# Expert tiles of the last routing round in pairs that share their weights, and a second table pass for the rest, in a two-layer Perceiver kernel

## The chip, the cores and the metric

The kernel runs on one core of a Trainium2 chip, as one program. Five engines take part, each with its own instruction queue that is worked in order: TensorE (PE, matrix products; its weight loads are listed as PEld), VectorE (DVE), ScalarE (ACT), GpSimd (POOL) and SyncE (SP, which here only issues DMAs). PE reads its operands from the on-chip buffer SBUF and writes to PSUM; DMAs move data between HBM and SBUF. The metric is the device time of one execution in microseconds; lower is better. The kernel before took 1743.54 us, the median of three runs (1740.70 to 1745.26).

## What is computed

4096 tokens (128 batches of 32) of 256 numbers go through six residual steps: cross attention to a context of 257 rows per batch, causal self attention, a feed-forward net with ternary weights, a second cross attention with 16 heads, local attention over five neighbours, and at last a mixture of experts. The change is in the last step alone. Cut to what matters it is:

```python
logits = x_flat @ router_w.T                     # 8 experts
top_v, top_i = top_k(softmax(logits), 2)         # two experts per token
top_v = top_v / sum(top_v)
for k in range(2):
    pos = (how many tokens before this one chose the same expert as their k-th)
    keep = pos < C                               # C = int(1.25 * 4096 / 8 * 2) = 1280
    expert_in[expert, pos] = layernorm(x)[token] if keep
    h = gelu(expert_in @ w1[expert])             # 256 -> 1024
    y = h @ w2[expert]                           # 1024 -> 256
    out[token] += gate * keep * y
```

All of it is in float32; the weights of one expert are two matrices of 1 MB.

## The kernel before

**Groups and lanes.** The 4096 tokens are 32 groups of 128. `group(g)` is a generator that brings one group through the five first steps and the router. Six lanes of buffers let six groups be in flight at a time.

**The order of the work** is found when the program is built. `Order` holds a set of such generators ("threads"). Each yields what it wants next: a slot of a buffer pool (`Slots`), a delay in ns, another thread's end, or an instruction block with an engine and an estimated duration. `Order.run` takes again and again the block that could begin first by these estimates, breaks ties by rank, and writes its instructions out. So the estimates (`LAG`, the price of a change of ScalarE's function table `TABLE` and `SWITCH`, `EARLY` and `LAND` for DMAs) decide the order of instructions on every engine; at run time the engines keep that order and wait for each other by semaphores. `keep_busy` puts in a few products that nobody reads where PE would idle long.

**Routing.** After every few groups (`TOGETHER`: seven times four, then two, one and one) `route(r)` finds the two experts of each token, ranks the tokens of an expert by products with a triangular matrix (`ranks`, the tile `chosen`), and works out a place in a list for each token. POOL writes (token number, gate) with an indirect DMA into the list `slot_ids` in HBM, a scatter for each of the two choices and each group. Every 128 places of an expert's list are one expert tile. `rounds_of_tiles` says how many tiles each round may start: 1, six times 8, 4, 2 and 17, together 72, whatever the routing is; `tiles_of_round` works out on VectorE which expert and which 128 places each tile of the round has (`i_exp`, `i_row`). In the last round also tiles that are not full are taken.

**An expert tile** (`expert_tile`, lines 1371 to 1453 of the kernel before) does this:

- `both_weights` takes two buffers of 1 MB from `halves_w` and POOL gathers the expert's `w1_moe` and `w2_moe` rows into them. There are three such buffers (`w`) while groups are running; when the context buffers `kT` and `kn` are used no more, six more are made of them, nine in all.
- POOL gathers the 128 list entries (`ids`), then the 128 token rows (`xt`, from `x_rows` in HBM).
- PE transposes the rows (L1408), ACT or DVE copies them to `xTm`.
- PE computes the hidden layer in two halves, each 4 blocks x 2 products of 128 columns, each followed by a Gelu on ACT (L1430) into `hT`.
- PE multiplies back: 8 products of 256 columns into one PSUM tile; ACT or DVE scales by the gate (`y`, L1449 and L1450).
- POOL scatters `y` to `out` with an add (L1129).

`xTm` and `hT` together are one slot of `rows_mid`, of which there are two, so two tiles can be between transpose and the end of the second product. There are three `xt`, eight `ids` and two `y` buffers, and four PSUM tiles.

**Locks.** Scatters and gathers of one HBM table are kept apart in the plan by the locks `at_slots`, `at_rows` and `at_out`. `locked` and `read` take the lock, then wait `EARLY` = 2500 ns, then issue; `locked` holds it for `LAND` = 4000 ns more. These are numbers of the plan; at run time POOL waits for the earlier DMA's semaphore.

A matmul in float32 of this kernel appears as two records in the trace. Line 357 (365 after the change) is the helper `matmul`, which records all products, so the groups are told apart by their tiles: `ps<-xTm,w` (or `kT`, `kn`) is the hidden layer, `ps<-w,hT` the second product.

## Time and profile before

| | |
|---|---|
| median of three runs | 1743.54 us |
| profiled execution, its own time | 1740.96 us |
| its span in the trace | 1739.3 us |
| mean granted TensorE clock | 0.957 |
| PE, DVE, ACT, POOL busy | 1574.5, 996.4, 1005.1, 773.8 us |
| DMA, mean over the span | 193 GB/s |
| last rank matmuls of the last round begin | 1520.8 us |
| last matmul ends | 1728.0 us |

The profile is of one execution; all stretches are us from the start of its span. A line of time order has start, duration, engine, line, operation, tiles written and read, partitions by elements, the count of merged instructions, and in brackets how long the engine was idle before it and what ended that, inferred from semaphore events. Where the named engine had long been done, something else was waited for, often a DMA. PE's busy time counts a record as busy from its start to its modelled end; consecutive records overlap, so pace is read from start to start. POOL's indirect DMAs are busy for as long as POOL writes out their descriptors; the data lands later.

### The profile page before, as it was taken

The numbers are of one execution on the slowest core, as the hardware profiler recorded it, in microseconds if no ns is written. First come the engines' busy times: TensorE is split into PE (matmuls) and PEld (weight loads), VectorE is DVE, ScalarE is ACT, GpSimd is POOL, SyncE is SP. The second block draws the span as 40 slices with busy tenths as digits, with TensorE's granted clock in tenths as the row PEclk, the third lists the DMA queues.
The fourth block names the chain that finished last, engine by engine and source line by source line (L and its number), as shares of the span: only waits on it lengthen the run. The fifth ranks groups of instructions, "written<-read, shape, count | busy, mean of one in ns | idle before, by whom it ended". The sixth has DMA issues, their size and how long they took to land. (4 is left out here: it accounts for less than half of the span.)

```text
span 1739.3 us, 43252 instructions
## 1 busy us (share of the span) xinstructions
PE 1574.5 (91%) x16702; PEld 1236.5 (71%) x16702; DVE 996.4 (57%) x3554; ACT 1005.1 (58%) x2649; POOL 773.8 (44%) x1026
## 2 busy tenths in 40 slices
PE   6988888899889999999999999999998998888987
PEld 5655656566667777767676777767776787877976
DVE  4685758777876776675667655775667443320000
ACT  1466655558666776756676666767666654312221
POOL 3221223333345435455444553454444555576763
PEclk8997989899999999999999999999999899989999
DMA  8562345353366566555655756646753357688984
GB/s 303 181 232 85 107 149 184 117 189 111 110 218 202 162 218 228 190 185 179 208 184 181 261 187 203 200 152 216 244 171 129 131 183 271 195 271 279 302 290 124
DMA packets 133150, 336.39 MB, mean 193 GB/s; under 512 B 17744, under 2 KB 43344, under 8 KB 114256
## 3 DMA queue, kind: packets, MB, share of 16 engines
q0 software_dynamic: 41984, 179.40, 31.3%
q1 hardware_dynamic: 90816, 154.09, 27.0%
q8 instruction: 132, 2.16, 0.5%
q14 instruction: 74, 0.61, 0.1%
q10 hardware_dynamic: 144, 0.13, 0.0%
HBM read 309.68 MB, written 23.87 MB: 192 GB/s over the span
## 5 line engine op out<-in xcount | busy, mean ns | idle before, releaser
L520 POOL TENSOR_SCALAR rstd<-mv 128x1 f32<-128x1 f32 x192 | 47.5, 248 | 477.9 <-DVE mv L515 357.3
L965 ACT ACTIVATE probs<-sps,nm 128x256 f32<-128x256 f32 x512 | 241.3, 484 | 29.1 <-DVE nm L921 21.1
L357 PEld LDWEIGHTS ps<-xTm,w 128*128 128x128 f32 x1632 | 209.0, 195 | 30.3 <-issue 13.5
L357 PE MATMUL ps<-xTm,w 128*128 128x128 f32 x1632 | 225.8, 283 | 5.0 <-issue 2.0
L357 PE MATMUL ps<-w,hT 128*128 128x256 f32 x768 | 203.2, 389 | 2.7 <-DVE qb L1085 1.3
L1430 ACT ACTIVATE hT<-ps 128x512 f32<-128x512 f32 x144 | 85.7, 597 | 196.5 <-PE ps L357 125.6
L919 DVE TENSOR_REDUCE nm<-sps 128x2 f32<-128x512 f32 x256 | 164.0, 683 | 34.4 <-PE sps L357 28.2
L583 PE MATMUL sps<-ident,probs 128*128 128x128 f32 x1024 | 156.9, 286 | 21.0 <-ACT probs L965 15.7
L493 ACT COPY probsT<-sps 128x512 f32<-128x512 f32 x238 | 137.7, 598 | 51.8 <-PE sps L583 45.3
L357 PEld LDWEIGHTS ps<-w,hT 128*128 128x128 f32 x768 | 134.1, 191 | 33.9 <-issue 16.6
L583 PEld LDWEIGHTS sps<-ident,probs 128*128 128x128 f32 x1024 | 120.1, 146 | 47.7 <-ACT probs L965 36.1
L1129 POOL DMA_INDIRECT out<-y,ids x72 | 117.7, 1635 | 69.5 <-ACT y L1450 33.1
L1124 POOL DMA_INDIRECT w<-in_w_moe,i_exp x99 | 101.5, 1025 | 95.1 <-PE ps L357 77.1
L493 ACT COPY xnT<-ps 128x256 f32<-128x256 f32 x173 | 64.0, 376 | 113.0 <-PE ps L535 94.0
L357 PE MATMUL sps<-probsT,kn 128*32 128x64 f32 x4096 | 108.0, 227 | 11.7 <-ACT probsT L493 6.8
L521 POOL TENSOR_TENSOR rstd<-rstd,mhalf 128x1 f32<-128x1 f32 x192 | 110.7, 577 | 16.0
L965 ACT ACTIVATION_READ_ACCUMULATOR probs<-sps,nm 128x1 f32 x512 | 109.2, 213 | 0.0
L357 PEld LDWEIGHTS sps<-probsT,kn 128*32 128x32 f32 x4096 | 71.9, 111 | 49.8 <-issue 32.2
L357 PE MATMUL sps<-kT,wide 32*64 32x256 f32 x2048 | 94.6, 420 | 6.9 <-DVE aT L998 6.8
L524 DVE TENSOR_SCALAR xn<-x,mv,rstd 128x256 f32<-128x256 f32 x175 | 72.5, 416 | 36.3 <-POOL rstd L521 35.4
L535 PE MATMUL ps<-ident,xn 128*128 128x128 f32 x384 | 76.5, 286 | 14.4 <-DVE xn L524 7.8
L1124 POOL DMA_INDIRECT xt<-x_rows,ids x72 | 71.7, 996 | 36.3 <-issue 14.0
(304 smaller groups left out, 3500.5 us busy)
## 6 DMA issues: line engine op xcount, KB each, us to landing
kT<-in_ctxT SPq DMA_DIRECT2D x256, 257.0 KB
kn<-in_ctx SPq DMA_DIRECT2D x256, 256.0 KB
x<-in_x SPq DMA_DIRECT2D x32, 128.0 KB
last<-in_ctx_last SPq DMA_DIRECT2D x32, 128.0 KB
out<-x POOLq DMA_DIRECT2D x32, 128.0 KB
x_rows<-xn POOLq DMA_DIRECT2D x32, 128.0 KB
x_rows<-nothing SPq DMA_DIRECT2D x7, 512.0 KB
w<-in_w SPq DMA_DIRECT2D x2, 1024.0 KB
```

The lines of the kernel that those rows point to most:

```text
L357: nc.tensor.matmul(out, lhsT=lhsT, rhs=rhs, **how)
L493: ("ACT", 60 + 0.815 * n, lambda: nc.scalar.copy(out, in_)),
L520: nc.gpsimd.tensor_scalar(rstd, mv[:, 1:2], EPS, None, ALU.add)
L521: nc.gpsimd.tensor_tensor(rstd, rstd, mhalf, ALU.pow)
L524: yield either(326, 1250, lambda e: e.tensor_scalar(xn, xg, mv[:, 0:1], rstd, ALU.subtract, ALU.mult))
L535: nc.tensor.transpose(pt[:, c, :], x[:, c * P : (c + 1) * P], ident)
L583: nc.tensor.transpose(by_key[:, i, c, :], e[:, i * LK + c * P : i * LK + (c + 1) * P], ident)
L919: nc.vector.tensor_reduce(nm[:, :, r], sps[r].rearrange("p (j k) -> p j k", j=2), AX.X, ALU.max)
L965: lambda: nc.scalar.activation(e[:, (2 * i + j) * LK : (2 * i + j + 1) * LK], sps[r][:, j * LK : (j + 1) * LK], AF.Exp, bias=nm[:, j, r : ...
L1124: nc.gpsimd.indirect_dma_start(out=dst, out_offset=None, in_=src, in_offset=bass.IndirectOffsetOnAxis(ap=idx, axis=0))
L1129: nc.gpsimd.indirect_dma_start(out=dst, out_offset=bass.IndirectOffsetOnAxis(ap=idx, axis=0), in_=src, in_offset=None, compute_op=op)
L1430: yield act(495, lambda: nc.scalar.activation(hT[:, 4 * half : 4 * half + 4, :].rearrange("p f t -> p (f t)"), hps, AF.Gelu), "gelu")
```

## The change

The last round's 17 tiles are no longer all alike. `rounds_of_tiles` now gives for each round a list of passes of (size, count). All rounds but the last have one pass of size 1. The last has two: four units of size 2, then nine of size 1; 8 + 9 tiles as before. A unit of size 2 (a "two" here) is 256 consecutive places of one expert.

- `tiles_of_round` runs its table of tiles once per pass. For size 2 it counts whole pairs of an expert's remaining tiles (`twos`), and makes two row indices per unit. After each pass it takes what was given out off `full`. Each pass's units are started by the new `begun`, when the slot scatters are in the plan (`sent`).
- `expert_tile` becomes `expert_tiles`. Each unit gathers the weights once. Each of its one or two sets of rows has its own id gather, row gather, transpose and copy, into one `xTm` of 256 columns. The hidden layer of a two is 16 products of 256 columns, with a Gelu after each 512 columns; the second product is done for each 128 rows, 2 x 8 products of 256 columns, side by side in one PSUM tile; two `y`, two scatters.
- Buffers: `rows_mid` are two `xTm` alone, twice as wide; `hT` becomes `hidden_of`, three halves of a hidden layer, each twice as wide, and a tile takes two of them, one when each half begins. The zero tile `nothing` is now borrowed from the `y` buffers.
- The plan: `SWITCH` 1000 to 700; `EARLY` is waited before a lock is asked for, not under it; the lags between a tile's PE blocks are 0 in the last round and 300 ns in the others (300 and 400 before).

```diff
-    per, most, pairs = [], 0, 0
-    for n in together:
+
+
+
+    per, did, pairs = [], 0, 0
+    for r, n in enumerate(together):
         pairs += 2 * n * P
-        full = max(0, pairs // TS - E + 1)
-        per.append(full - most)
-        most = full
-    per[-1] += 2 * E - 1
+        full = max(0, pairs // TS - E + 1) - did
+        if r == len(together) - 1:
+            full += 2 * E - 1
+            two = max(0, (full - E) // 2)
+            per.append([(2, two), (1, full - 2 * two)])
+        else:
+            per.append([(1, full)])
+        did += sum(size * n for size, n in per[-1])
+        per[-1] = [p for p in per[-1] if p[1]]
...
-    SWITCH = 1000.0
+    SWITCH = 700.0
...
-    rows_mid = Slots(
-        [(keep.tile([P, 2, TS], F32, name=f"xTm{i}"), keep.tile([P, 8, TS], F32, name=f"hT{i}")) for i in range(2)]
-    )
+    rows_mid = Slots([keep.tile([P, 2, 2 * TS], F32, name=f"xTm{i}") for i in range(2)])
+
+    hidden_of = Slots([keep.tile([P, 4, 2 * TS], F32, name=f"hT{i}") for i in range(3)])
...
     def locked(lock, engine, ns, emit):
 
+        yield EARLY
         yield lock
-        yield EARLY
         yield [(engine, ns, emit, None, LAND)]
         order.give(lock, None)
...
-        table = order.thread(tiles_of_round(r), order.now.rank)
+        sent = Mark()
+        table = order.thread(tiles_of_round(r, sent), order.now.rank)
         for i in range(RB):
             for k in range(2):
                 yield from locked(
                     at_slots, "POOL", 1000, lambda: scatter(slot_ids, islot[:, k, i : i + 1], ids[:, k, i, :])
                 )
         yield table
-        i_row, i_exp = table.made
-        rounds_done.append(
-            [
-                order.thread(expert_tile(r, t, i_row[:, t : t + 1], i_exp[:, t : t + 1]), tile_rank(r, t))
-                for t in range(ROUNDS[r])
-            ]
-        )
+        sent.end()
...
-        yield from steps("DVE", (850, there), (1640, sums), (1000, which), (1150, first_slots), (1290, weights))
-        order.now.made = i_row, i_exp
+        yield from steps("DVE", (850, there))
+        for size, n in ROUNDS[r]:
+            te = [P, n, E]
+            past, one = (work.tile([P, NT, E], F32, name=f"t_{x}")[:, 0:n] for x in ("past", "one"))
+            row, some = (work.tile([P, NT], F32, name=f"t_{x}")[:, 0:n] for x in ("row", "some"))
+            at_i = work.tile([P, size + 1, n], I32, name=f"at_{r}_{size}")
+            i_row, i_exp = at_i[:, 0:size], at_i[:, size : size + 1]
+            over = lambda t: t.unsqueeze(1).to_broadcast(te)
+            tiles = iota_t[:, 0:n].unsqueeze(2).to_broadcast(te)
+
+            def sums():
+                units = full
+                if size == 2:
+
+                    units = twos
+                    nc.vector.tensor_scalar(twos, full, 0.5, -0.25, ALU.mult, ALU.add)
+                    nc.vector.tensor_scalar(twos, twos, MAGIC, MAGIC, ALU.add, ALU.subtract)
+                nc.vector.tensor_copy(upto, units)
...
+                    nc.vector.scalar_tensor_tensor(row, some, float(TS), row, ALU.mult, ALU.add)
+                    nc.vector.tensor_scalar(i_row[:, 1], row, iota_p, float(NOBODY), ALU.add, ALU.add)
...
+                nc.vector.tensor_tensor(took, took, twos if size == 2 else full, ALU.min)
+                nc.vector.scalar_tensor_tensor(done, took, float(size), done, ALU.mult, ALU.add)
+                nc.vector.scalar_tensor_tensor(full, took, -float(size), full, ALU.mult, ALU.add)
+
+            yield from steps(
+                "DVE", (1640 + 150 * (size - 1), sums), (1000, which), (1150 + 150 * (size - 1), first_slots), (1360, weights)
+            )
+            order.thread(begun(r, t, size, n, i_row, i_exp, sent), order.now.rank)
+            t += size * n
+
+    def begun(r, t, size, n, i_row, i_exp, sent):
+        yield sent
+        for i in range(n):
+            order.thread(
+                expert_tiles(r, t + size * i, [i_row[:, k, i : i + 1] for k in range(size)], i_exp[:, 0, i : i + 1]),
+                tile_rank(r, t + size * i),
+            )
...
     def read(lock, dst, src, idx):
+        yield EARLY
         yield lock
-        yield EARLY
         yield [("POOL", 1000, lambda: gather(dst, src, idx), None, 0.0)]
         order.give(lock, None)
         yield LAND
...
+        N = len(i_rows)
+        between = 0.0 if r == len(ROUNDS) - 1 else 300.0
+        mid, ids = [], []
+
+        def rows_of(i):
+            mine = yield ids_of
+            yield from read(at_slots, mine, slot_ids, i_rows[i])
+            xt = yield rows_in
+            yield from read(at_rows, xt, x_rows, mine[:, 0:1])
+            ids[i] = mine
+            if i == 0:
+                mid.append((yield rows_mid))
+                known.end()
+            else:
+                yield known
+            xT = mid[0]
+            ps = yield ps_g
+            pt = ps[:, 0:D].rearrange("p (c t) -> p c t", c=2)
+
+            def turn():
+                for c in range(2):
+                    nc.tensor.transpose(pt[:, c, :], xt[:, c * P : (c + 1) * P], ident)
+
+            yield pe(221, turn)
+            order.give(rows_in, xt)
+            yield copy(xT[:, :, i * TS : (i + 1) * TS], pt, D)
+            order.give(ps_g, ps)
+
+        read_by, known = [], Mark()
+        for i in range(N):
+            ids.append(None)
+            read_by.append(order.thread(rows_of(i), order.now.rank))
+        for x in read_by:
+            yield x
+        xT = mid[0]
         yield loaded
         yield landed[0]
         wk = w1[0].rearrange("p (kc f) -> p kc f", kc=2)
+        M = N * TS
+        each = 512 // M
+        hT = []
         for half in range(2):
-            hps = yield ps_g
-            for f in range(0, 4, 2):
-                def hidden():
-                    for i in range(2):
-                        n = f + i
-                        products(
-                            hps[:, n * TS : (n + 1) * TS],
-                            [(wk[:, kc, (4 * half + n) * P : (4 * half + n + 1) * P], xT[:, kc, :]) for kc in range(2)],
-                        )
-
-                yield pe(888, hidden)
-            yield act(495, lambda: nc.scalar.activation(hT[:, 4 * half : 4 * half + 4, :].rearrange("p f t -> p (f t)"), hps, AF.Gelu), "gelu")
-            order.give(ps_g, hps)
+            hT.append((yield hidden_of))
+            for b in range(0, 4, each):
+                hps = yield ps_g
+                for f in range(0, each, 3 - N):
+
+                    def hidden():
+                        for n in range(f, f + 3 - N):
+                            at = (4 * half + b + n) * P
+                            products(
+                                hps[:, n * M : (n + 1) * M], [(wk[:, kc, at : at + P], xT[:, kc, 0:M]) for kc in range(2)]
+                            )
+
+                    yield [("PE", 757 if N == 2 else 888, hidden, None, 300.0 if f + 3 - N == each else between)]
+                out_h = hT[half][:, b : b + each, 0:M]
+                in_h = hps.rearrange("p (f t) -> p f t", f=each)
+                yield act(495, lambda: nc.scalar.activation(out_h, in_h, AF.Gelu), "gelu")
+                order.give(ps_g, hps)
         order.give(halves_w, w1[0])
+        order.give(rows_mid, xT)
         yield landed[1]
         wf = w2[0].rearrange("p (fc d) -> p fc d", fc=8)
         yps = yield ps_g
-        for f in range(0, 8, 2):
-            def back():
-                for fc in range(f, f + 2):
-                    matmul(
-                        yps[:, 0:D], lhsT=hT[:, fc, :], rhs=wf[:, fc, :], start=fc == 0, stop=fc == 7
-                    )
-
-            yield [("PE", 757, back, None, 400.0)]
+        for i in range(N):
+            for f in range(0, 8, 2):
+
+                def back():
+                    for fc in range(f, f + 2):
+                        matmul(
+                            yps[:, i * D : (i + 1) * D], lhsT=hT[fc // 4][:, fc % 4, i * TS : (i + 1) * TS], rhs=wf[:, fc, :],
+                            start=fc == 0, stop=fc == 7,
+                        )
+
+                yield [("PE", 757, back, None, 400.0 if f == 6 else between)]
         order.give(halves_w, w2[0])
-        order.give(rows_mid, mid)
-        y = yield rows_out
-        gate = ids[:, 1:2].bitcast(F32)
-        yield [
-            ("DVE", 395, lambda: nc.vector.tensor_scalar(y, yps[:, 0:D], gate, None, ALU.mult)),
-            ("ACT", 372, lambda: nc.scalar.mul(y, yps[:, 0:D], gate)),
-        ]
-        order.give(ps_g, yps)
-        yield from locked(at_out, "POOL", 1620, lambda: scatter(out, ids[:, 0:1], y, ALU.add))
-        order.give(rows_out, y)
-        order.give(ids_of, ids)
+        for h in hT:
+            order.give(hidden_of, h)
+
+        def sent_back(i):
+            y = yield rows_out
+            gate, in_y = ids[i][:, 1:2].bitcast(F32), yps[:, i * D : (i + 1) * D]
+            yield [
+                ("DVE", 395, lambda: nc.vector.tensor_scalar(y, in_y, gate, None, ALU.mult)),
+                ("ACT", 372, lambda: nc.scalar.mul(y, in_y, gate)),
+            ]
+            left.append(i)
+            if len(left) == N:
+                order.give(ps_g, yps)
+            yield from locked(at_out, "POOL", 1620, lambda: scatter(out, ids[i][:, 0:1], y, ALU.add))
+            order.give(rows_out, y)
+            order.give(ids_of, ids[i])
+
+        left = []
+        for i in range(N):
+            order.thread(sent_back(i), order.now.rank)
```

## The prediction

> **What bounds the kernel now.** I read the page first, for the engine shares over the span, then the sums by stage, then the order of time on TensorE and on GpSimd in the last 220 us, where the changed round lies.
>
> ```profile
> span 1739.3 us, 43252 instructions
> PE 1574.5 (91%) x16702; PEld 1236.5 (71%) x16702; DVE 996.4 (57%) x3554; ACT 1005.1 (58%) x2649; POOL 773.8 (44%) x1026
> ```
>
> ```profile
> 1200.00:1300.00 100.00, 96.36 (x1042) 76.20 (x1041) 61.31 (x198) 67.31 (x168) 43.83 (x59) 0.98 0.62 203
> ...
> 1600.00:1650.00 50.00, 48.70 (x326) 44.51 (x325) 0.48 (x1) 12.46 (x26) 35.06 (x33) 1.00 0.92 307
> ...
> 1521.00:1541.00 20.00, 13.21 (x72) 11.38 (x72) 9.42 (x52) 2.84 (x6) 15.65 (x15) 0.80 0.88 292
> 1541.00:1600.00 59.00, 53.76 (x357) 49.30 (x356) 0.00 (x0) 12.53 (x27) 38.24 (x35) 0.95 0.80 261
> ...
> 1521.00:1728.00 207.00, 189.14 (x1225) 171.57 (x1224) 9.90 (x53) 45.64 (x97) 129.77 (x119) 0.96 0.81 265
> ```
>
> (The second fence is the sums by stage. Its columns: its stretch, its length, busy time of PE, weight loads, DVE, ACT, POOL, then granted clock, DMA share, GB/s.) TensorE is the bound: 96 of 100 us in the middle, 48.7 of 50 at 1600. After the last router (1521) only expert tiles are left: VectorE and ScalarE are nearly idle, while PE, POOL and DMA all run near their limits, and PE loses 18 us idle and more at a clock of 0.80 to 0.95.
>
> ```profile
> 1509.55 0.59 POOL L1100 DMA_DIRECT2D out<-x x1
> 1510.13 0.20 POOL L1186 IOTA tok_ids<- 128x32 int32 x1
> 1517.60 1.64 POOL L1129 DMA_INDIRECT out<-y,ids  x1 [7.26 <-ACT hT L1430]
> ...
> 1549.65 0.99 POOL L1129 DMA_INDIRECT slot_ids<-tok_ids,islot  x1 [0.30 <-issue]
> ...
> 1559.07 0.99 POOL L1129 DMA_INDIRECT slot_ids<-tok_ids,islot  x1 [0.30 <-issue]
> ...
> 1727.67 1.55 POOL L1129 DMA_INDIRECT out<-y,ids  x1 [2.89 <-issue]
> 1732.13 1.55 POOL L1129 DMA_INDIRECT out<-y,ids  x1 [2.91 <-issue]
> ```
>
> ```profile
> 1537.37 3.78 PE L357 MATMUL ps<-kn,hT 128*128 128x256 f32 x8 [6.79 <-ACT hT L1430]
> ...
> 1577.09 1.80 PE L357 MATMUL ps<-xTm,kn 128*128 128x128 f32 x8 [4.37 <-ACT xTm L493]
> ...
> 1715.36 1.03 PE L357 MATMUL ps<-kT,hT 128*128 128x256 f32 x4
> 1716.23 1.05 PE L357 MATMUL ps<-xTm,kT 128*128 128x128 f32 x8
> 1717.12 0.38 PE L1408 MATMUL ps<-ident,xt 128*128 128x128 f32 x2
> 1717.34 1.89 PE L357 MATMUL ps<-kT,hT 128*128 128x256 f32 x8
> ```
>
> The reader should see, in GpSimd's order, that a scatter into `out` stood 7.26 us behind the direct write of `out` just before it; everything queued after it, weight gathers too, came late. In PE's order: the stalls of 6.79 and 4.37 us that follow (the activation named had long been done; a gather was late), the first eight matmul records after 4.37 us taking 1.59 us to the next group (1577.09 to 1578.68) instead of 0.89, and the regular pace: four records of 256 columns (two matmuls) in 0.87 us (1715.36 to 1716.23), eight of 128 columns (four matmuls) in 0.89 us.
>
> From these a tile costs PE 16 x 0.222 + 8 x 0.434 + 2 x 0.11 = 7.24 us. POOL needs four gathers at 1.26 us (0.95 busy, 0.30 between) and a scatter at 1.9, 6.9 us. Two weight gathers are 2 x 128 rows x 8 KB = 2.1 MB, the rows in and out add some 0.27: 2.37 MB at 307 GB/s over a DMA share of 0.92, 334 GB/s, are 7.1 us. All three within 0.4 us: any slip on POOL or DMA reaches PE. In the order on PE, 177.3 us of work at that pace stand after the last router's rank matmuls; they took 1521.5 to 1728.0, 206.5 us. **29 us are lost there**, and this is what the change can reach.
>
> **The change, part by part.**
>
> *Matmul work.* In each of the four twos, the first product of two tiles, 32 x 0.222 = 7.10 us, becomes 16 x 0.434 = 6.94 us: -0.16, four times -0.6 us. The second product is as before. The Trainium skill ("TensorE: Matmul & The Clock Gate", Back-to-back issue gap) gives 81 ns a matmul at 128 columns and 131 at 512, so that widening would be almost free: interpolated, an estimate of some 98 ns at 256 columns, 0.60 of the time for the same columns, and 4 x 2.8 = 11 us off. The rows above, 0.222 against 0.434 us, say that time goes with columns here, and the sum uses them.
>
> *Weight traffic.* Eight of 144 gathers go: 8.4 MB, 25 us of DMA at 334 GB/s and 8 x 1.26 = 10 us of POOL, both in the stretch where they bind. In a two, the DMA time for 14.3 us of PE work falls from 14.2 to 7.9 us and POOL's from 13.9 to 11.4; with four twos first, the nine weight buffers of the tail are refilled ahead of the nine single tiles. So stalls like those after 1560 (4.37, 2.11 and two near 1.1 us, with their slow clock some 14 us of the 29) should mostly go.
>
> *What stands ahead of the twos.* On PE 52 of the 72 row transposes stand before the last rank matmuls instead of 49, and 157.4 us of work behind them instead of 177.3. This moves 20 us ahead of the last router; PE being 96% busy there, the router comes later by as much: 0, or a gain where it fills idle time (10 of 91 us between 1430 and 1521). I take -2, bounds 0 and -10.
>
> *The new chain.* Behind the rank matmuls PE has 31.4 us of queued work before the first two's transpose; the kernel before has six tiles queued, and its first last-round transpose comes 71 us after (at 1592.42). By the rows the chain is: slots known after 4.0 us (1520.8 to 1524.8), then GpSimd's order from the first slot scatter to the second row gather: two slot scatters, four weight gathers, three output scatters, five id gathers, two row gathers, 2 x 1.3 + 11 x 1.26 + 3 x 1.9 = 22.2 us, and 2.7 us to land (the wait from 1729.22 to 1731.91): 28.9 us. It fits with 2.5 us to spare. Each wait of a scatter for an earlier one's landing (4.4 us apart at the end) goes beyond that. I take a stall of 4 us, bounds 0 and 20. The direct write of `out` is now followed by two gathers before the next scatter into it, so 2.5 of the 7.26 us of blocking is covered: I take 8 us for all other losses of the tail. Tail losses 29 to 12: **-17 us**.
>
> *End of the kernel.* The last three outputs came 2.8 us apart and queued behind each other's landing: the last scatter began at 1732.13, y having been ready at 1728.5. In the new order two hidden steps (1.8 us) and a whole second product (3.5 us) lie between the last two outputs, 5.3 us, more than the 4.4 of a scatter: -2.5 us.
>
> *Tables.* The second pass adds some 7 us of small VectorE operations (the first took 1524.8 to 1532.0), when VectorE has nothing else (0.48 us between 1600 and 1728), and its nine tiles start 50 us of PE work after the first two: 0. Each earlier round gains one operation of 0.17 us: 0. Without the cover of the twos it would be 7 us.
>
> *Planner.* A switch price of 0.7 us instead of 1.0, and the 2.5 us delay taken before a lock instead of under it, reorder all engines. Table loads go from 152 to 158: 6 x 1.28 = 7.7 us of ScalarE, 58% busy; I take +2 of 0 to 7.7. The delay no longer widens the time between two writes of one DRAM table; waits of POOL for such landings (17 us for `slot_ids` and ids together, in the waits) may grow, or tiles may fill PE better. Nothing in the trace prices a new order: 0, with 12 us either way, about a third of PE's idle time between 600 and 1300.
>
> *Sum.* -0.6 -17 -2 -2.5 +2 = -20.1 us. Profiled execution 1740.96 (span 1739.3 and 1.66 around it): 1720.9. It stood 2.6 us under the median of 1743.54: **1723.5**.
>
> **The rivals.**
> A. *Losses move, not vanish* (within 0.3%, some 1741): PE's work is the same to 0.6 us, and the order before 1521 gives back 12 us while the chain stalls 10: 1743.5 - 20.1 + 12 + 6 = 1741. For it: PE at 96% in the middle; against it: DMA and POOL, not PE, made the 29 us.
> B. *The first two's rows come late* (slower): GpSimd's in-order queue holds them behind scatters, and PE runs dry. If they come as late as the first last-round rows of before, 71 us after the ranks, PE idles 40 us instead of 4: 1723.5 + 36 = 1760. It decides from 31.4 + 4 + 20 = 55 us on. For it: the 7.26 us wait, three output scatters in the chain. Against it: 8 GpSimd operations now stand between the last router's iota and the first slot scatter, 22 before.
> C. *The middle gains too*: the earlier tiles fill idle time for the full 12 us and the filler 6 more: 1705.
> That twos would not form cannot be: their count is fixed when the program is built.
>
> **How the numbers follow.** Forecast 0.48 (its own range 1712 to 1735), A 0.14, B and other losses of a new order 0.22, C 0.16. A measurement tells 0.3%, 5 us, from no change. Faster 0.48 + 0.16 = 0.64, same 0.14, slower 0.22. The range goes to 1706 and 1752: outside lie the far half of C and most of B, near 2 in 10.
>
> **What would show it.** Right: from the last rank matmuls to the last matmul some 170 us instead of 206.5, DMA share under 0.75 there, no PE stall over 2 us once the twos run, the first transpose of a two 31 to 36 us after the ranks, the last scatter within 2 us of the last PE end. Wrong: the last router over 25 us later than 1521, or a PE stall over 15 us before the first two.
>
> The clock is a second witness: the Trainium skill (same page, Part 1: The HAM clock gate) says that the array is slowed when it has lately been idle; 0.80 in the 20 us with the 6.79 us stall agrees.

## The result and the profile after

The changed kernel takes **1776.66 us** (median of four runs, 1771.94 to 1778.17) against 1744.38 us for the kernel before (four runs). The ratio is 1.0176, 95% interval 1.0158 to 1.0193: slower by 1.8%, where 1723.5 us was forecast.

The page of the changed kernel, its span and engine line:

```profile
span 1773.7 us, 43056 instructions
...
PE 1575.7 (89%) x16549; PEld 1246.3 (70%) x16586; DVE 1015.0 (57%) x3634; ACT 1013.9 (57%) x2638; POOL 752.8 (42%) x1003
```

TensorE (PE) has the same 1575 us of busy time as before, in a span that is 34.4 us longer. The sums by stage (columns as in the prediction's second fence) of the changed kernel:

```profile
1200.00:1300.00 100.00, 93.63 (x1014) 73.94 (x1015) 62.48 (x226) 69.14 (x170) 43.29 (x53) 0.98 0.61 201
1599.00:1766.00 167.00, 160.87 (x965) 145.49 (x963) 15.82 (x89) 41.08 (x84) 98.15 (x88) 0.99 0.71 222
```

The middle, 96.4 us busy of 100 before, is at 93.6. The stretch from the last rank matmuls (now at 1598.88) to the last matmul runs at a clock of 0.99, where it had 0.96, and with a DMA share of 0.71 instead of 0.81. In PE's order of time there (changed kernel):

```profile
1598.88 0.51 PE L365 MATMUL ps<-chosen,before 128*128 128x8 f32 x4
...
1630.86 2.05 PE L365 MATMUL ps<-xTm,kn 128*128 128x128 f32 x16 [0.85 <-ACT hT L1498]
1632.75 0.38 PE L1462 MATMUL ps<-ident,xt 128*128 128x128 f32 x2
1636.87 1.39 PE L365 MATMUL ps<-kT,hT 128*128 128x256 f32 x4 [3.74 <-ACT hT L1498]
...
1652.63 3.72 PE L365 MATMUL ps<-kn,hT 128*128 128x256 f32 x16 [1.06 <-ACT hT L1498]
...
1676.11 1.89 PE L365 MATMUL ps<-xTm,w 128*128 128x256 f32 x8
1677.84 1.89 PE L365 MATMUL ps<-xTm,kT 128*128 128x256 f32 x8
```

The first two's rows are transposed 33.9 us after the ranks (1632.75), PE stalls 3.74 us before the second set, and once the twos run nothing over 1.06 us remains. GpSimd's last scatters of the changed kernel:

```profile
1757.92 1.57 POOL L1137 DMA_INDIRECT out<-y,ids  x1 [3.32 <-ACT hT L1498]
1762.51 1.55 POOL L1137 DMA_INDIRECT out<-y,ids  x1 [3.02 <-issue]
1766.88 1.55 POOL L1137 DMA_INDIRECT out<-y,ids  x1 [2.82 <-ACT y L1525]
```

The last begins 1.2 us after the last matmul (1765.7); it was 4.1 us. So the end of the kernel got shorter by about what was forecast. The time was lost ahead of it:

| from the trace, us | before | after | difference |
|---|---|---|---|
| last rank matmuls of the last round | 1520.8 | 1598.9 | +78.1 |
| row transposes issued by then (of 72) | 49 | 52 | +3 |
| PE idle until then | 135.5 | 184.0 | +48.5 |
| PE at half clock until then | 122.9 | 170.7 | +47.8 |
| last ranks to last matmul | 207.2 | 166.8 | -40.4 |
| last matmul to end of span | 11.3 | 8.0 | -3.3 |

Three more tiles ahead of the last ranks explain 20 of the 78.1 us, and 20 of the 40.4. What remains is +58 before the ranks, -20.4 and -3.3 after them: +34. ("At half clock" is the time in which the trace's records of the granted clock show about half.) An example of how a stall costs twice, in PE's order of the changed kernel:

```profile
1577.43 0.69 PE L1462 MATMUL ps<-ident,xt 128*128 128x128 f32 x2 [7.66 <-DMA xt<-x_rows,ids]
1577.91 1.91 PE L365 MATMUL ps<-xTm,w 128*128 128x128 f32 x8
1579.62 1.92 PE L365 MATMUL ps<-xTm,kT 128*128 128x128 f32 x8
1581.33 1.86 PE L365 MATMUL ps<-xTm,w 128*128 128x128 f32 x8
1583.02 1.06 PE L365 MATMUL ps<-xTm,kT 128*128 128x128 f32 x8
1583.91 1.46 PE L365 MATMUL ps<-kn,hT 128*128 128x256 f32 x6
```

After 7.66 us without work, three groups of eight records take 1.71, 1.71 and 1.69 us, start to start; the next takes 0.89.

### The profile page after: what moved, and what is told of

It is laid out like the page before. It is cut to its first block, busy times and chain, and to the rows that moved or that the text cites. A ratio compares the mean times of both kernels' runs of the same rounds, so it can differ in the third digit from the quotient of the medians.

```text
span 1773.7 us, 43056 instructions
## 1 busy us (share of the span) xinstructions
PE 1575.7 (89%) x16549; PEld 1246.3 (70%) x16586; DVE 1015.0 (57%) x3634; ACT 1013.9 (57%) x2638; POOL 752.8 (42%) x1003
## 5 line engine op out<-in xcount | busy, mean ns | idle before, releaser
L365 PE MATMUL ps<-xTm,w 128*128 128x128 f32 (+1 forms) x1600 | 226.4, 286 | 1.5 <-ACT xnT L501 1.0
L365 PEld LDWEIGHTS ps<-xTm,w 128*128 128x128 f32 x1600 | 206.3, 194 | 22.6 <-issue 10.1
L365 PE MATMUL ps<-w,hT 128*128 128x256 f32 x816 | 211.7, 389 | 4.4 <-ACT hT L1498 2.0
L927 DVE TENSOR_REDUCE nm<-sps 128x2 f32<-128x512 f32 x256 | 164.4, 684 | 47.8 <-PE sps L365 39.2
L365 PEld LDWEIGHTS ps<-w,hT 128*128 128x128 f32 x816 | 143.8, 191 | 36.1 <-issue 12.6
L591 PEld LDWEIGHTS sps<-ident,probs 128*128 128x128 f32 x1024 | 122.9, 149 | 53.5 <-ACT probs L973 37.1
L1132 POOL DMA_INDIRECT w<-in_w_moe,at x100 | 102.4, 1024 | 103.9 <-PE ps L365 71.9
L1137 POOL DMA_INDIRECT slot_ids<-tok_ids,islot x64 | 68.6, 1072 | 51.3 <-issue 11.5
```

The source lines that it names most:

```text
L365: nc.tensor.matmul(out, lhsT=lhsT, rhs=rhs, **how)
L591: nc.tensor.transpose(by_key[:, i, c, :], e[:, i * LK + c * P : i * LK + (c + 1) * P], ident)
L927: nc.vector.tensor_reduce(nm[:, :, r], sps[r].rearrange("p (j k) -> p j k", j=2), AX.X, ALU.max)
L1132: nc.gpsimd.indirect_dma_start(out=dst, out_offset=None, in_=src, in_offset=bass.IndirectOffsetOnAxis(ap=idx, axis=0))
L1137: nc.gpsimd.indirect_dma_start(out=dst, out_offset=bass.IndirectOffsetOnAxis(ap=idx, axis=0), in_=src, in_offset=None, compute_op=op)
```

## The experiments

The eighteen runs below fell on five chips. The kernel before takes 1673 to 1675 us on four of them (B, D, E, F) and 1739 on C; the first pair of kernels ran on a chip that the record does not name, called the first chip here, where it took 1744 (it may have been C). So a ratio is always against the kernel before on the same chip, and stretches are compared within a chip where there is a pair. Times are us; idle, half clock and the last two columns are from the profiled execution, idle and half clock up to its last matmul.

| run | chip (before, us) | us | ratio, 95% interval | PE idle, all | half clock, all | last ranks | last ranks to last matmul |
|---|---|---|---|---|---|---|---|
| e1 change without twos | B 1675 | 1717.2 | 1.0251 [1.0220, 1.0282] | 148 | 120 | 1539.5 | 167.2 |
| e2 change, lock order back | B | 1687.1 | 1.0078 [1.0051, 1.0105] | 128 | 102 | 1497.9 | 176.9 |
| e3 change, SWITCH back | B | 1685.7 | 1.0064 [1.0041, 1.0086] | 127 | 102 | 1508.5 | 164.5 |
| e4 change, both back | B | 1690.1 | 1.0097 [1.0067, 1.0127] | 127 | 102 | 1476.3 | 193.5 |
| e5 before again | C 1739 | 1741.2 | 1.0008 [0.9981, 1.0036] | 154 | 143 | 1525.0 | 203.6 |
| e6 change again | C | 1770.8 | 1.0178 [1.0123, 1.0234] | 179 | 195 | 1595.6 | 169.1 |
| e7 before, early wait | C | 1794.2 | 1.0291 [1.0229, 1.0352] | 182 | 225 | 1581.0 | 206.3 |
| e8 before, SWITCH 700 | C | 1746.7 | 1.0038 [1.0011, 1.0066] | 155 | 147 | 1540.5 | 196.6 |
| e9 twos alone | D 1673 | 1675.6 | 1.0008 [0.9994, 1.0021] | 120 | 99 | 1467.5 | 189.8 |
| e10 the same, early wait in last round | D | 1673.3 | 0.9994 [0.9977, 1.0011] | 121 | 92 | 1464.9 | 191.8 |
| e11 before, another lag | D | 1681.9 | 1.0056 [1.0039, 1.0073] | 122 | 102 | 1485.6 | 181.3 |
| e12 before, both constants | D | 1685.5 | 1.0077 [1.0062, 1.0093] | 132 | 102 | 1501.5 | 173.8 |
| e13 before again | E 1674 | 1674.8 | 1.0006 [0.9986, 1.0027] | 116 | 102 | 1469.3 | 188.7 |
| e14 twos alone again | E | 1673.6 | 0.9989 [0.9971, 1.0006] | 117 | 99 | 1466.6 | 189.4 |
| e15 as e10 | E | 1673.0 | 0.9992 [0.9971, 1.0013] | 117 | 102 | 1471.2 | 191.3 |
| e16 change again | E | 1718.9 | 1.0246 [1.0200, 1.0292] | 149 | 147 | 1546.4 | 164.6 |
| e17 change, tiles held | F 1673 | 1710.3 | 1.0232 [1.0191, 1.0274] | 151 | 123 | 1495.8 | 206.6 |
| e18 before, tiles let go | F | 1677.4 | 1.0029 [1.0008, 1.0050] | 124 | 109 | 1503.1 | 164.5 |

On the four faster chips the span of the profiled execution less the idle time and less half of the half-clock time is 1497 to 1510 us in every row (e13: 1672.3 - 116 - 51 = 1505; e16: 1718.8 - 149 - 73 = 1497). So on them these two columns account for what differs to within some 13 us. On the first chip they would give 72 us ahead of the ranks for the 58 found. Most of the other 14 was counted twice, since part of the half-clock time passes while PE is idle anyway: of PE's busy time up to the last ranks 102.3 us ran at half clock before and 132.0 after, worth 15 us rather than 24, and 48 and 15 make 63.

### Twos or plan? (e1 to e4)

```diff
 # e1: the same tiles and passes, no unit of two
-            per.append([(2, two), (1, full - 2 * two)])
+            per.append([(1, 2 * two), (1, full - 2 * two)])
 # e2, in locked() and read()
-        yield EARLY
         yield lock
+        yield EARLY
 # e3
-    SWITCH = 700.0
+    SWITCH = 1000.0
 # e4: e2 and e3
```

> The changed kernel, with the last round's two passes kept but both of single tiles (8, then 9): weights are gathered for each tile again, all else as in the changed kernel. Order up to the last router is the same as in the changed kernel. Theory N (new order: the loss of 32 us comes from PE idle time before the last router, made by the new order of the plan; the twos only shorten the tail): slower than the changed kernel by 10 to 22 us, 1787 to 1799 us, the extra behind the last rank matmuls. Theory T (the twos themselves, their larger steps and three half buffers, cost the time): back to 1740 to 1755 us.

> The changed kernel with the 2.5 us delay taken under a lock again, as before the change; twos and a switch price of 0.7 us stay. Theory L (the delay before the lock makes the plan place tile work earlier than its data comes, and in-order engines then stall): the loss goes, 1715 to 1735 us, with PE idle before the last router back at some 137 us. Theory C (chance: any new order loses some 1 to 3% against an order whose constants were picked on the chip): 1755 to 1790 us. Theory S (the switch price): no change, 1777 us.

> The changed kernel with the planner's switch price back at 1.0 us; the delay stays before the lock. Theory S (the lower price makes ScalarE change tables too often): 1720 to 1740 us. Theory L: no change, 1765 to 1785 us. Theory C: 1755 to 1790 us, either side of the changed kernel.

> The changed kernel with both planner constants as before (switch price 1.0 us, delay under the lock): the twos, the second table pass, the buffers and the step lags alone. Theories L and S: 1715 to 1735 us, the tail's gain of some 17 us without the loss. Theory C: 1755 to 1790 us although both constants are back, because buffers and lags have changed the order too.

Without the twos the loss stays (1.0251; the whole change is at 1.0246 on chip E, where the kernel before takes the same time), so they don't make it; nor did the 10 to 22 us more come that theory N expected of leaving them out. Undoing either constant of the plan gives back 69 to 75% of it (2.51% to 0.78 and 0.64), undoing both no more than either (0.97%): the two don't add. So neither theory L nor S holds by itself; theory C's range, 0.6 to 2.6% above the kernel before, holds all three. With both back the buffers and lags still give another order than that of before, and it is 1% slower. How much of that 1% is the order, and how much the new buffers themselves (three halves of a hidden layer where two whole ones stood), no run separates; PE's waits for hidden layers (`ps` for `hT` from ScalarE) sum to the same 3.6 us in e13 and e16, so the buffers do not show there.

### One constant each on the kernel before (e5 to e8)

```diff
 # e7: the kernel before, EARLY before the lock
-        yield lock
         yield EARLY
+        yield lock
 # e8: the kernel before
-    SWITCH = 1000.0
+    SWITCH = 700.0
```

> The kernel before, unchanged, for a profile on the same chip as the runs beside it; the first four experiments ran on a chip where it took 1675 us. Ratio to before 1.000 within 0.3%. Theory C: its PE idle time before the last rank matmuls is lower, at equal tile work done, than that of any variant.

> The changed kernel, unchanged. Ratio 1.013 to 1.021 if the chip does not matter. If the stall of 10 us on all engines at 1097 us of its first profile was an accident of that execution, it is not there at the same place; if it belongs to the program, it is.

> The kernel before, its single tiles and buffers kept, with the 2.5 us delay taken before the lock. Theory L: slower by 1.5 to 2.5%. Theory C: slower too, by anything from 0.3 to 2.5%, and no more than the next one. If neither this nor the next is slower than before by 0.3%, the constants are not the cause and buffers or lags are.

> The kernel before with only the planner's switch price at 0.7 us. Theory L: within 0.3% of before. Theory C: slower by 0.3 to 2.5% although nothing but one number of the plan has changed, and the loss is PE idle time before the last rank matmuls.

The wait before the lock alone costs 2.9%, more than the whole change on this chip (1.8%); the switch price alone 0.4%. That misses both theories: 2.9% lies above L's range and C's, and C wanted it no higher than the switch price. e7 shows where the time goes: against e5, idle time grows by 28 us and half-clock time by 82. The result of the change itself repeats on this chip (e6, 1.0178), and the kernel before against itself is at 1.0008 (e5).

### The twos alone (e9, e10), a neutral re-plan (e11), both constants (e12)

In e9 and e10 the plan puts out the very order of the kernel before up to the last round's table; only the last round differs. e11 changes a number that has nothing to do with tiles.

```diff
 # e9: the kernel before, and
+    two = max(0, (per[-1] - E) // 2)
+    per[-1] = [(2, two), (1, per[-1] - 2 * two)]
...
+        if r == len(ROUNDS) - 1:
+            table = order.thread(last_tiles(r, sent), order.now.rank)
 # e10: e9, and for the last round's tiles alone
+        if first:
+            yield EARLY
         yield lock
-        yield EARLY
+        if not first:
+            yield EARLY
 # e11: the kernel before
-    LAG = {"PE": 300.0, "DVE": 130.0, "ACT": 150.0, "POOL": 90.0, "SP": 3500.0}
+    LAG = {"PE": 300.0, "DVE": 120.0, "ACT": 150.0, "POOL": 90.0, "SP": 3500.0}
 # e12: e7 and e8
```

> The kernel before, with the last round's four twos and nine singles (two table passes, weights read once per two, xTm twice as wide, one spare hT; the lags of a tile's PE blocks 0 in the last round), and nothing else: SWITCH 1000, EARLY under the lock, rows_mid in pairs as before. The planned order is the order of before on every engine until the last round's table begins, so the last ranks must come where they come in before, within its own scatter. Theory P (the twos bring what was forecast, and the whole loss is the new order of the earlier rounds): from the last ranks to the last matmul 207 us become 185 to 195, ratio 0.987 to 0.994. Rival T (the twos themselves or the second table pass cost time as well): ratio 1.000 or above, with a stall of PE before the first two or between the passes.

> As the run before it, and EARLY is also waited before the lock, but only by the tiles of the last round: gathers and scatters of the last round are planned closer together, the order before the last ranks is still that of before. Theory P: the early wait harms through the earlier rounds alone, here it does no harm and may take off 0 to 5 us more in the tail: ratio 0.985 to 0.994. Rival W (the early wait is bad in itself, it lets POOL's queue fill with scatters that wait for landings): a ratio above that of the run before it by 0.005 or more.

> The kernel before with one number of the plan changed that has nothing to do with the change: the lag after a VectorE block, 130 to 120 ns. Work and buffers are the same; the planned order parts from that of before early. Theory O (the order of before is an unusually good one, and nearly any other order of the same work costs time): ratio 1.004 to 1.03, with more idle and half-clock time of PE before the last ranks. Rival E (only what the two edits of the plan do costs time): ratio 0.997 to 1.003.

> The kernel before with both edits of the plan (SWITCH 700, EARLY before the lock) and no twos. If the two effects add (2.9 and 0.4 per cent alone): ratio 1.028 to 1.038. Theory O (each new order is its own case): anywhere from 1.004 to 1.03, not predictable from the two alone. Theory P wants it above 1.010, since the change without its twos was at 1.025.

Theory P's second half fell: the twos are worth nothing on this chip. Rival W fell too, as e10 is no slower than e9. Theory O held in the ratio: ten nanoseconds in an unrelated lag cost 0.56%, and both constants together 0.77%, far under the 3.3% of their sum (on another chip), and under the 1.0% that theory P wanted. The idle and half-clock time that O wanted ahead of the last ranks is hardly there in e11: 115 and 99 us, against 111 and 99 in e13, on another chip of the same time.

### Pairs on one chip (e13 to e16)

> The kernel before again, for a profile on the same chip as the next three. Ratio 0.998 to 1.002. If the losses of its last stretch (29 us of 207 on the first chip) belong to that chip's slower transfers, then on a chip with some 1675 us this stretch is about 190 to 195 us, and on one with some 1740 us about 203 to 208 us.

> The twos on the order of before, as run before on a chip with 1673 us (1.0008). Theory D (the twos save weight traffic, and are worth what the transfers cost PE in the last stretch): on a chip with some 1740 us the last stretch is 8 to 17 us shorter than that of the run before this one, ratio 0.990 to 0.996; on a chip with some 1675 us it is 0 to 5 us shorter, ratio 0.997 to 1.002. Rival T (the twos are worth nothing anywhere): ratio 0.998 to 1.003 on either.

> The same with the early wait for the tiles of the last round alone. As the run before it, and the end of the kernel 2 to 6 us closer to the last matmul: theory D 0.986 to 0.995 on a chip with some 1740 us, 0.995 to 1.001 on one with some 1675 us. Rival T: 0.996 to 1.003.

> The changed kernel, for a profile on the same chip as before. Theory P (its whole loss lies in the order of the earlier rounds): its last ranks come 60 to 80 us later than those of the first of these four runs, and its last stretch is 25 to 40 us shorter, 20 us of it being three tiles that it did earlier; ratio 1.010 to 1.030. Rival Q (the loss belongs to the chips with some 1740 us alone): ratio under 1.010 on a chip with some 1675 us.

The sums by stage on chip E, from the second rank matmuls to the seventh, on to the last, and on to the last matmul. The kernel before (e13):

```profile
434.00:1279.00 845.00, 809.80 (x9430) 632.01 (x9429) 584.73 (x2070) 594.88 (x1562) 411.41 (x545) 0.99 0.62 201
1279.00:1469.00 190.00, 183.37 (x1824) 155.94 (x1824) 97.49 (x410) 113.69 (x262) 110.62 (x120) 0.99 0.61 206
1469.00:1658.00 189.00, 183.73 (x1230) 169.25 (x1228) 10.03 (x53) 47.20 (x97) 129.18 (x118) 0.99 0.89 290
```

The changed kernel (e16):

```profile
428.00:1359.00 931.00, 882.72 (x9948) 693.36 (x9948) 607.28 (x2142) 636.60 (x1634) 432.31 (x562) 0.98 0.61 200
1359.00:1546.00 187.00, 160.06 (x1443) 136.24 (x1444) 87.14 (x377) 84.98 (x204) 105.30 (x116) 0.92 0.55 181
1546.00:1711.00 165.00, 160.94 (x967) 146.29 (x965) 15.64 (x89) 41.48 (x83) 100.29 (x91) 0.99 0.74 234
```

The twos alone (e14), last ranks to last matmul:

```profile
1467.00:1656.00 189.00, 180.81 (x1097) 162.88 (x1096) 14.34 (x86) 46.57 (x98) 121.09 (x110) 1.00 0.77 245
```

The loss of the changed kernel lies before the last ranks on this chip too, most densely where the last groups run out: 27 us idle of 187 at a clock of 0.92, against 7 of 190 at 0.99. From e13 to e16 the last ranks move by +77.1 us (33.7 more idle, 44.4 more at half clock, 20 of tiles done earlier: 33.7 + 22.2 + 20 = 76), the stretch behind them by -24.0 and the end by -6.6; +46.5 in all. Theory P's marks were met but for the stretch, where 25 to 40 was forecast, and rival Q fell.

The last stretch of e14 moves 16% less per second than that of e13 (245 against 290 GB/s) and is as long, 189.4 against 188.7 us. The old tail lost only 11 us here (188.7 less 177.3 of work), with the same DMA load as on the first chip: 0.89 of 189 us and 0.81 of 207 us are both 168 us. So there the traffic hid behind PE, as theory D says; but D's "slower transfers" as the reason for the first chip's 29 us have no support in this, and what makes its tail lose more is open. Nor did a run of the twos alone come to such a chip. A sign that the twos may be worth something there is in the table: on the first chip and on C the tails that follow 49 tiles, without twos, lose 19 to 30 us (the kernel before, e5, e7, e8, less 177.3 of work), those of the changed kernel 9 and 12 (the result and e6, less 157.4). But these differ in order as well, so it is not shown.

The start of the first chip's stalls, as the prediction read it, does not hold up either. GpSimd's order in the kernel before on chip E (e13):

```profile
1458.08 0.58 POOL L1100 DMA_DIRECT2D out<-x  x1
1458.66 0.19 POOL L1186 IOTA tok_ids<- 128x32 int32 x1
1466.05 1.64 POOL L1129 DMA_INDIRECT out<-y,ids  x1 [7.20 <-ACT hT L1430]
```

The scatter stands behind the direct write for 7.20 us as it did for 7.26, and yet this is PE's longest stall in the whole stretch (e13):

```profile
1533.73 2.05 PE L357 MATMUL ps<-xTm,kn 128*128 128x128 f32 x8 [2.16 <-DMA kn<-in_w_moe,i_exp]
```

The first chip had 6.79 and 4.37, and chip C has 9.29 at the same products (e5, at 1544.1). So that wait alone does not make the stalls.

What PE waited for, summed over the run, the first and some other lines. The kernel before (e13):

```profile
PE sps L583 <- ACT probs L965: 14.2, 25, 1.9
PE ps L535 <- DVE xn L524: 8.1, 8, 3.8
...
PE ps L1408 <- DMA xt<-x_rows,ids: 1.6, 2, 1.3
```

The changed kernel (e16):

```profile
PE ps L1462 <- DMA xt<-x_rows,ids: 20.7, 7, 8.4
PE sps L591 <- ACT probs L973: 17.1, 24, 1.9
PE ps L543 <- DVE xn L532: 13.7, 12, 3.8
```

(Total us, times, longest.) The new first line is a tile's transpose that waits for its token rows: 19 of the 33 us by which idle time grew. In the profile of the result itself this line is smaller, 8.1 us against none before, of 36 more idle in all; there the waits for VectorE's `aT` grew more, from 6.8 to 20.3, 10.24 of it in one stall (last section). The longest, in the order of GpSimd (e16):

```profile
1502.16 0.95 POOL L1132 DMA_INDIRECT xt<-x_rows,ids  x1 [0.30 <-issue]
1507.26 0.59 POOL L1111 DMA_DIRECT2D x_rows<-xn  x1 [4.15 <-DMA xt<-x_rows,ids]
...
1515.10 0.96 POOL L1132 DMA_INDIRECT ids<-slot_ids,at  x1 [1.43 <-DMA slot_ids<-tok_ids,islot]
...
1519.06 0.99 POOL L1137 DMA_INDIRECT slot_ids<-tok_ids,islot  x1 [1.10 <-DMA ids<-slot_ids,at]
...
1522.89 0.95 POOL L1132 DMA_INDIRECT xt<-x_rows,ids  x1 [0.30 <-issue]
```

and what followed on PE and ScalarE (e16):

```profile
1530.18 0.69 PE L1462 MATMUL ps<-ident,xt 128*128 128x128 f32 x2 [8.44 <-DMA xt<-x_rows,ids]
...
1530.91 0.37 ACT L501 COPY xTm<-ps 128x256 f32<-128x256 f32 x1 [8.65 <-PE ps L1462]
...
1543.82 0.20 ACT L1211 ACTIVATE ex<-ex 128x1 f32<-128x1 f32 x1
```

GpSimd waits for landings on the two tables in turn, 6.7 us in three places, the row gather behind them begins 21 us after the one before it, PE idles 8.44 us. ScalarE, in its own order, waits 8.65 us for that transpose, and the last routing's exponent stands further back in the same queue: its input was there at 1507.7, it runs at 1543.8 (in e13 1456.2 and 1466.9). In the re-planned orders run here this wait for rows sums to 2 to 21 us, in the kernel before (three profiles) to 0 to 1.6. The distance of the gathers alone is not enough: in e13 two row gathers stand 27 us apart (1449.18 and 1476.28), and PE, with other tiles queued, then waits 1.28 us. That GpSimd's order makes the rows of this one tile late is read from these lines; that the late rows are what a new order costs was not isolated by a run.

### Is it filler? (e17, e18)

The changed kernel has started 39 tiles by the seventh ranks, the kernel before 34, so fewer are left to fill PE where the groups run out.

```diff
 # e17: the changed kernel; the sixth round's tiles two groups later
-            after += 0
+            after += 2
 # e18: the kernel before
-        after = sum(TOGETHER[: r + 1]) + 0 + (t + 0) // 2
+        after = sum(TOGETHER[: r + 1]) + 0
```

> The changed kernel, with the tiles of the sixth round (the fifth from the end) let go two groups later. The planned order is that of the changed kernel up to the sixth last rank matmuls' stage; then 35 instead of 39 tiles stand before the seventh ranks. Theory F (tiles done too early are missing as filler where the groups run out, PE idles there and its clock is halved after it): between the seventh and the last rank matmuls idle falls from 27 to under 12 us and half-clock time from 31 to under 10 us on a chip with some 1675 us (from 35 and 41 to some 20 and 20 on one with 1740 us), ratio 1.004 to 1.013. Rival G (the loss is spread over the whole order, filler or not): idle stays above 20 us there, ratio 1.016 or above.

> The kernel before, with no tile held back for a group: all tiles of a round may begin when the round's table is known. 38 instead of 34 tiles stand before the seventh rank matmuls, 52 instead of 49 before the last. Theory F: idle between the seventh and the last rank matmuls rises from 7 to 15 to 25 us on a chip with some 1675 us (from 20 to 30 or more on one with some 1740 us), with as much half-clock time, ratio 1.010 to 1.025. Rival G: idle there stays within 3 us of that of before and the ratio is whatever the other stages give, 1.000 to 1.010.

Seventh to last ranks of e17, to be set beside the second line of e16:

```profile
1335.00:1496.00 161.00, 149.70 (x1486) 124.93 (x1488) 86.82 (x386) 91.96 (x223) 99.37 (x109) 0.99 0.60 197
```

The filler does what theory F says in its place: idle there falls from 27 to 11 us, half-clock time from 31 to 3 (rival G wanted over 20 us idle). But the ratio stays at 1.0232: idle opens where the tiles were taken away (8 to 14 us in the stage before) and in the last stretch, now four tiles longer (4 to 13 us). e18 has 15 us idle there for 7, again as F says and not as G does, and loses 0.3%, not 1 to 2.5. So F is right about the place and fell as the cause of the whole: in both runs the ratio is G's. What is gained in one stretch comes back in others, so the time is best read as one of the whole order; which of its features costs most stays open.

## Why the prediction was wrong

- *The bound and the tail.* Right on the first chip. The tail's losses fell from 29 to 9 us (166.8 less 157.4 of work): -20 for the -17 forecast. The marks given for it were met: 170 us forecast and 166.8 measured from the last ranks, a DMA share under 0.75 (0.71), the first transpose after 31 to 36 us (33.9), no stall over 2 us in the twos (1.06), the last scatter within 2 us of PE's end (1.2). But on chip E the twos alone shortened nothing, and e1, without twos, has a tail of 167.2 us as well (on chip B). So how much of the first chip's 20 belongs to the twos, and how much to the order or to the chip, is not shown. The reading that the 7.26 us behind the direct write of `out` made the stalls is not borne out: e13 has nearly the same wait without them.
- *Matmul work, -0.6.* Right: eight records of 256 columns take 1.73 us, start to start (1676.11 to 1677.84), 0.433 us a matmul. The near-flat pace that the Trainium skill gives ("TensorE: Matmul & The Clock Gate", Back-to-back issue gap: 81 ns at 128 columns, 131 at 512) does not hold for these float32 products, which take 0.222 us at 128.
- *The new chain, a stall of 4 us.* Right: 0.85 + 3.74.
- *End of the kernel, -2.5.* It measured -3.3, but not because of the twos, so here the number was luck. In the ten profiles where `EARLY` is waited before the lock in the last round, 7.6 to 8.2 us pass after the last matmul, with single tiles too (e7, 8.2, against e5, 11.2); in the ten others 11.2 to 14.3, with twos too (e14, 13.9). In e10 and e15 the end is 6 us shorter than in e9 and e14 and the stretch before it 2 us longer; what is left is within the noise of the ratios (0.9994 and 0.9992).
- *What stands ahead of the twos, -2; bounds 0 and -10.* Wrong in sign as far as it can be told: idle time was not filled. Up to the seventh ranks five tiles more are now done, and between the second and the seventh idle time went from 48 to 79 us.
- *Planner, "0, with 12 us either way".* This is the step that failed: **+58 us**. The bound, a third of PE's idle time between 600 and 1300, was taken from the idle time that is there, which limits what an order can gain and not what it can lose. What the runs showed in its place: new orders of the same work alone cost 0.4 to 2.9% (e7, e8, e11, e12), the twos on the old order nothing (e9, e14). It also left out the clock: from e13 to e16, 34 us more idle ahead of the ranks came with 44 us more at half clock, worth 22. The Trainium skill (same page, Part 1: The HAM clock gate) says that the clock depends on how busy PE has been recently; the lines at 1577.43 agree, 1.71 us for 0.89 after 7.66 us without work. The table loads, +2 in the sum, rose from 152 to 158 as forecast; what they cost was not isolated, but they are not the cause, as e2 has 168 and loses 0.78%.
- *The rivals.* B ended on the right side with the wrong place: the first two's rows were not late, those of tiles before the last ranks were. A's give-back of 12 us by the order named the right place at a fifth of its size. The mark set for "wrong", the last router over 25 us later, is what came: 78, or 58 without the three tiles.
- Nine re-plans were run beside the change's own (e2 to e4, e7, e8, e11, e12, e17, e18), and all are slower than the old order, by 0.3 to 2.9%. No version was found that is faster than the kernel before; the twos on the old order (e10, e15) are level with it.

## What to carry to other kernels

Where a planner writes the order of a whole kernel, a constant of the plan is not a local edit: split such a change, keep the old order up to the changed part (e9), and price the constants as a new draw of the order, by runs. Don't bound its loss by the idle time that is there now, and look at the granted clock behind each new stall: PE's work at half clock added 15 us to 48 of idle on the first chip, and some 22 to 34 on chip E. A saving of transfers is worth only what they cost the bound engine: 8.4 MB less were worth nothing on chip E, where the tail lost 11 us.

## What had not been expected of the hardware

- The same kernel takes 1673 to 1675 us on four chips, 1739 on C and 1744 on the first. The slower ones have more PE idle time (154 us in e5 against 116 in e13) and more half-clock time (143 against 102), with the same bytes (336.39 MB) and much the same DMA time in the tail (0.82 of 204 us and 0.89 of 189).
- The amount of half clock that comes with idle time differs between orders: from none (e12 against e13, on another chip of the same time: 15 us more idle, 0 more) to three times the idle time (e7 against e5: 28 and 82).
- In the profiled run of the change PE stalled 10.24 us at 1108.2 with VectorE and ScalarE idle with it; the same order stalled 8.31 us at the same instruction on chip C (e6, at 1103.7), and not at all there on chips B (e1) and E (e16). What held the engines is not shown by any record, and it stays open.
